# Nine Toeplitz products a head instead of ten, and two sums of each chunk pair on GpSimd

## The chip, the core and the metric

The kernel runs on one core of a Trainium2 chip, as one launch. The metric is the device time of the launch in microseconds (us). The engines are PE (TensorE, matmuls), DVE (VectorE), ACT (ScalarE), POOL (GpSimd) and SP (SyncE, which issues most of the DMAs). Each works through its own queue in order.

## What is computed

The input x has the shape (8, 256, 512), the context as well. Layer one is a causal long convolution with a product structure; layer two is a mixture of 16 experts with four experts a token, plus a shared expert. With k = v = context and q = layernorm(x), and 32 heads of 8 rows:

```python
kv = jnp.einsum('bhil,bhjl->bijhl', k_, v_)
y = jnp.fft.irfft(jnp.fft.rfft(kv, n=2 * L) * kernel_f, n=2 * L)[..., :L]
out = jnp.einsum('bijhl,bhil->bjhl', y + kv * D[None, None, None, :, None], q_)
x = x + out
x = x + ffn(layernorm(x))   # shared expert and 4 of 16 experts, each a gated silu
```

The convolution along L = 512 is causal. Cut into four chunks of 128, it is a lower triangular block Toeplitz product: with T0 to T3 the four 128 x 128 blocks of one head and K0 to K3 the chunks of kv, chunk c of y is the sum over m from 0 to c of Tm times K(c-m). That is 1 + 2 + 3 + 4 = 10 products.

## The kernel before

All is fp32. The attention part is one loop of 16 iterations over n. One iteration handles a tile of 128 rows (8 batches by 16 rows), which is two heads (HT = 2). Since k = v, only 288 of the pairs (i, j) are formed (PAIRS = 4 x 64 + 32), so one Toeplitz product is a 128x128 by 128x288 matmul.

- blocks (L345) loads the four Toeplitz blocks of a head from pad_d, a copy of the convolution kernel in device memory with 128 zeros ahead of it and D added to its first element. Partition p reads 512 consecutive values from an offset that grows by one with p. This is the DMA toep<-pad_d at L349: one contiguous piece of 2 KB for each partition. The blocks of an iteration are loaded by SP at the start of the one before; toep has four buffers.
- products (L354) forms kv on GpSimd: one instruction at L359 (128x128) and four at L361 (128x256) for a head. kv has four buffers.
- attend (L368) is called twice for a head, for chunks 0 and 1 (c0 = 0, three matmuls) and for chunks 2 and 3 (c0 = 2, seven). The matmuls at L381 accumulate in y, a PSUM tile with two buffers. DVE then multiplies y with q and sums over i: z at L393, L398 and L404, y in place at L409, f at L410, f with itself at L411 (128x256), and the sum into oT at L412 (128x128). y is free after L410; f and z have two buffers.
- add_to_x (L416) transposes oT of the iteration before on PE and adds it to x (L422). statistics (L262) runs on ACT with two small instructions on GpSimd, L273 and L274 (rstd); normalise (L290) is on ACT.
- From the fourth tile on, k and q of the next tile come in another layout through device memory: send_blocks (sent) and fetch_blocks (got) on SP, then a DVE transpose of 32 x 32 blocks (L327) and an ACT copy (L333). Up to the third tile, PE transposes them (heads_of, L336).
- by_feature (L440) computes the gate's logits of a finished tile on PE (L444), takes the four largest on DVE and counts selected tokens in early (L460, on DVE).
- shared_block (L137) is the shared expert as a generator; fill(count) runs so many of its pieces. These pieces (sgu at L163, sgt at L149, so at L180) are PE work put between the attends, and what is left of them after the loop runs on, before the experts start.

The order of each engine's instructions is the order in which the code issues them (manual_schedule over all engines). In an iteration that order is: DMA loads, attend(0, 0), fill, statistics of a later tile, attend(0, 2), add_to_x of the tile before, fill, the products of the next tile's head 0, attend(1, 0), fill, normalise and store of the tile before, the products of head 1, the gate of an older tile, attend(1, 2), fill, normalise of a later q.

PSUM is used in full: ps_mm two buffers for the shared expert, ps_tr two buffers (tag pt) for transposes and gate products, ps_y two of two banks each.

Of the kernel before, what the change touches and what calls it, by code (L numbers as in the profile page):

```python
# [20 lines left out]
P = 128  # L21
BK = 32
B, S, L = 8, 256, 512
HD = 8
# [12 lines left out]

ND = HD // 2
PAIRS = ND * HB + HB // 2
KW = HB + 3 * B  # L40
QW = HB + 4 * B
BACK = 2 * B
# [9 lines left out]
def ssm_attention__then__moe_kernel(  # L52
# [33 lines left out]

    xw_d = dram.tile([T + CAP, ROW], F32, name="xw_d")
    pad_d = dram.tile([S // HD, P + L], F32, name="pad_d")

    pad = const.tile([S // HD, P + L], F32, name="pad")
    dcol = const.tile([S // HD, 1], F32, name="dcol")
    nc.vector.memset(pad[:, 0:P], 0.0)
    nc.scalar.dma_start(out=pad[:, P:], in_=ssm)
    nc.scalar.dma_start(out=dcol, in_=skip)
    nc.vector.tensor_add(pad[:, P : P + 1], pad[:, P : P + 1], dcol)
    nc.scalar.dma_start(out=pad_d[:, :], in_=pad)  # L100
    ident = const.tile([P, P], F32, name="ident")
    make_identity(nc, ident)
    mhalf = const.tile([P, 1], F32, name="mhalf")
# [151 lines left out]
    with ExitStack() as att:  # L255
# [3 lines left out]
        work = att.enter_context(tc.tile_pool(name="work", bufs=2))  # L259
        ps_y = att.enter_context(tc.tile_pool(name="ps_y", bufs=2, space=PSUM))  # L260

        def statistics(dst, src, total=None):  # L262


            if total is None:
                total = small.tile([P, 1], F32, name="total")
                nc.scalar.activation(dst, src, AF.Identity, accum_out=total)
            neg = small.tile([P, 1], F32, name="neg")
            ss = small.tile([P, 1], F32, name="ss")
            rstd = small.tile([P, 1], F32, name="rstd")  # L270
# [73 lines left out]

        def blocks(head):  # L345

            toep = work.tile([P, L], F32, name="toep", bufs=4)
            row = pad_d[head : head + 1, 1 : 1 + L]
            nc.sync.dma_start(  # L349
                out=toep, in_=bass.AP(tensor=row.tensor, offset=row.offset, ap=[[1, P], [1, L]])  # L350
            )
            return toep

        def products(hh, k2):  # L354

            kv = work.tile([P, NC, PAIRS], F32, name="kv", bufs=4)
            kh = k2[:, :, hh, :]
            kc = kh.ap[1][0]
            nc.gpsimd.tensor_mul(kv[:, :, ND * HB :], kh[:, :, 0 : HB // 2], kh[:, :, HB // 2 : HB])  # L359
            for c in range(NC):  # L360
                nc.gpsimd.tensor_mul(  # L361
                    kv[:, c, 0 : ND * HB].rearrange("p (d w) -> p d w", d=ND),
                    kh[:, c, 0:HB].unsqueeze(1).broadcast_to([P, ND, HB]),
                    view(kh[:, c, :], 0, [[B, ND], [1, HB]]),
                )
            return kv

        def attend(hh, c0, toep, kv, q2, oT):  # L368

            qh = q2[:, :, hh, :]
            qc = qh.ap[1][0]
            y = ps_y.tile([P, 2, 512], F32, name="y")
            for i in range(2):
                c = c0 + i
                for m in range(c + 1):  # L380
                    nc.tensor.matmul(  # L381
                        y[:, i, 0:PAIRS],
                        lhsT=toep[:, m * P : (m + 1) * P],
                        rhs=kv[:, c - m, :],
                        start=(m == 0),
                        stop=(m == c),
                    )
# [15 lines left out]
            w = (ND - 1) * B  # L403
            nc.vector.tensor_mul(  # L404
                view(z, ZW, [[zc, 2], [ZW + B, ND - 1], [1, w]]),
                yd[:, :, 1:ND, HB - w : HB],
                qq[:, :, HB - w : HB].unsqueeze(2).broadcast_to([P, 2, ND - 1, w]),
            )
            nc.vector.tensor_mul(yd, yd, view(qq, 0, [[qc, 2], [B, ND], [1, HB]]))  # L409
            nc.vector.tensor_add(f, yd, z[:, :, :, BACK : BACK + HB])  # L410
            nc.vector.tensor_add(f[:, :, 0:2, :], f[:, :, 0:2, :], f[:, :, 2:4, :])  # L411
            nc.vector.tensor_add(  # L412
                oT[:, c0 : c0 + 2, hh * HB : (hh + 1) * HB], f[:, :, 0, :], f[:, :, 1, :]
            )

# [24 lines left out]
        def by_feature(n):  # L440
# [16 lines left out]

            if n == 0:
                nc.vector.memset(early[:, 0, :], 0.0)
            nc.vector.tensor_add(early[:, n + 1, :], early[:, n, :], sel[:, n, :])  # L460

        toeps = {}

# [29 lines left out]
        qn = load.tile([P, L], F32, name="qn", tag="kn")  # L493
        k2 = heads_of(loaded.pop(0), KW, "k2")
        stats = first_statistics(xs[:, 0, :])
        kvs = [products(0, k2)]
        normalise(qn, xs[:, 0, :], *stats)
        kvs.append(products(1, k2))
        q2 = heads_of(qn, QW, "q2")
        pg = ps_tr.tile([P, NC, P], F32, name="pg", tag="pt")  # L500
        for c in range(NC):
# [28 lines left out]
        for n in range(NT):  # L530
# [9 lines left out]
            if swift and more:  # L540
                got_k, got_q = fetch_blocks(sent_k), fetch_blocks(sent_q)
            load_shared(9)
            if n:
                attend(0, 0, tps[0], kvs[0], q2, oT)
            if n - 2 in MILD:
                transpose_blocks(xnT[:, :, n - 2, :], got_x)
            if more:
# [3 lines left out]
                        statistics(qn, xs[:, n + 1, :]) if n else first_statistics(xs[:, 1, :])  # L551
                    )
            if n == 0:
                attend(0, 0, tps[0], kvs[0], q2, oT)
            fill(2)
            if n + 2 in SWIFT:
                kp, kp_by_block = in_blocks("kp")
                kp_stats = statistics(kp_by_block, chunked(xs[:, n + 2, :]))

            attend(0, 2, tps[0], kvs[0], q2, oT)  # L560
            if more and not swift:
                k_next = heads_of(loaded.pop(n + 1), KW, "k2")
                normalise(qn, xs[:, n + 1, :], *stats)
# [5 lines left out]
            if more:  # L569
                if swift:  # L570
                    k_next = heads_from(got_k, KW, "k2")
                kv_next = [products(0, k_next)]

            attend(1, 0, tps[1], kvs[1], q2, oT)
            if more and not swift:
                q_next = heads_of(qn, QW, "q2")
            fill(2)
# [7 lines left out]
            if more:  # L585
                if swift:
                    q_next = heads_from(got_q, QW, "q2")
                kv_next.append(products(1, k_next))
            if n + 2 in SWIFT:
                nc.scalar.copy(kp_by_block, chunked(loaded.pop(n + 2)))  # L590
                sent_k = send_blocks(kp)
            if n - 2 in MILD:
                ready(n - 2)

            attend(1, 2, tps[1], kvs[1], q2, oT)
            if n - 1 in MILD:
                got_x = fetch_blocks(sent_x)
            elif n > 0:
# [320 lines left out]
```

## Time and profile before

| | |
|---|---|
| median of 3 runs | 717.03 us (716.22 to 719.62) |
| the profiled execution | 719.41 us |
| its span, first to last instruction | 717.7 us |
| mean granted TensorE clock | 0.99 |
| L361, products on GpSimd, 128x256, 128 of them | 698 ns median |
| L359, products on GpSimd, 128x128, 32 of them | 457 ns median |
| L409, y in place on DVE, 128x512, 64 of them | 700 ns mean |
| toep<-pad_d on SP, 32 of 256 KB | 4.8 us median from issue to landing |

The profiled execution's time is 1.7 us longer than its span, for what lies around the first and last instruction. The attention loop runs from about 11 to 370 us, what is left of the shared expert to about 445, the experts to the end. The first three iterations (to about 46 us) have little or no shared expert work to put between the attends. In the listings an instruction group is given as line, engine, operation, output<-inputs, shape and count, then busy time and the mean of one; answers for one line give the minimum, median and maximum instead.

### The profile page before, as it was taken

The page shows a single profiled execution, that of the slowest core. Times are in us where ns is not written, and L with a number is a line of the kernel's source. Part 1 is how long each engine was busy: PE and PEld are TensorE (multiplying, and loading weights), DVE is VectorE, ACT ScalarE, POOL GpSimd, SP SyncE. Part 2 cuts the span into 40 slices and gives each one's busy share as a digit, 9 for nine tenths or more (in the row PEclk, how much of TensorE's full clock was granted, in tenths as well). Part 3 has the DMA queues.
Part 4 walks back from the last instruction along what each step waited for, and adds up shares of the span by engine and source line. Part 5 has one row for each costly group of instructions (what it writes and reads, how often), then busy time and mean ns, then how long its engine had stood idle before and what let it go on. Part 6 is the DMA issues. An engine that isn't in the chain of part 4 may idle for free.

```text
span 717.7 us, 9733 instructions
## 1 busy us (share of the span) xinstructions
PE 692.0 (96%) x3471; PEld 521.5 (73%) x3471; DVE 402.3 (56%) x952; ACT 187.1 (26%) x472; POOL 211.8 (30%) x307
## 2 busy tenths in 40 slices
PE   5899999899999999999999999999999999999994
PEld 3677877787876886886876685777777677777772
DVE  3787767879987877778635511333333433443221
ACT  2353234352332351331122001121212221112120
POOL 5444224353333342133000020122332233332221
PEclk9999999999999999999999999999999999999997
DMA  7832453645556445541007431476677776777732
GB/s 202 290 89 75 118 148 80 175 126 158 144 155 162 108 117 143 148 106 55 16 16 241 116 86 30 133 213 182 182 192 219 213 193 185 200 203 207 195 42 32
DMA packets 76144, 102.17 MB, mean 142 GB/s; under 512 B 10224, under 2 KB 45040, under 8 KB 76096
## 3 DMA queue, kind: packets, MB, share of 16 engines
q1 hardware_dynamic: 68784, 84.35, 40.7%
q0 software_dynamic: 7168, 17.04, 11.6%
q8 instruction: 28, 0.46, 0.3%
q14 instruction: 20, 0.16, 0.1%
q10 hardware_dynamic: 144, 0.15, 0.1%
HBM read 74.02 MB, written 27.49 MB: 141 GB/s over the span
## 4 chain that ended last, share of the span: by engine, by line
PE 91%; DVE 4%; DMA 2%; issue 1%; ACT 1%; POOLq 0%; POOL 0%; ACTq 0%; DVEq 0%; SPq 0%
PE y L381 20%; PE sgu L163 19%; PE pgu L795 15%; PE eo L837 11%; PE so L180 11%; PE pgu L815 4%; PE pt L134 2%; PE pgu L807 2%; PE sgt L149 2%; PE lg L444 2%; PE ip L700 1%; PE pt L420 1%; DVE y L409 1%; DVE f L410 1%; DMA out<-eo_sb,idx 1%
## 5 line engine op out<-in xcount | busy, mean ns | idle before, releaser
L381 PE MATMUL y<-kv,toep 128*128 128x288 f32 x640 | 172.5, 419 | 3.0 <-DVE f L410 2.1
L381 PEld LDWEIGHTS y<-kv,toep 128*128 128x128 f32 x640 | 123.0, 196 | 41.2 <-issue 7.2
L795 PE MATMUL pgu<-xgT,w 128*128 128x256 f32 (+1 forms) x544 | 113.8, 367 | 0.8 <-ACT xgT L767 0.8
L795 PEld LDWEIGHTS pgu<-xgT,w 128*128 128x128 f32 x544 | 98.5, 190 | 20.4 <-issue 7.7
L361 POOL TENSOR_TENSOR kv<-k 128x256 f32<-128x256 f32 x128 | 88.9, 724 | 0.0
L837 PE MATMUL eo<-wd,mid 128*128 128x512 f32 (+1 forms) x192 | 86.4, 598 | 0.0
L846 POOL DMA_INDIRECT out<-eo_sb,idx x32 | 51.0, 1595 | 103.3 <-DMA out<-eo_sb,idx 73.2
L163 PE MATMUL sgu<-xnT,swg 128*128 128x256 f32 (+1 forms) x400 | 78.1, 338 | 2.4 <-DVE tail L157 2.4
L163 PE MATMUL sgu<-xnT,swu 128*128 128x256 f32 (+1 forms) x400 | 77.8, 337 | 0.0
L754 POOL DMA_INDIRECT g<-xw_d,idx x32 | 32.0, 999 | 150.7 <-PE eo L837 64.7
L180 PE MATMUL so<-swd,smid 128*128 128x512 f32 x160 | 74.4, 594 | 0.0
L273 POOL TENSOR_SCALAR rstd<-ss 128x1 f32<-128x1 f32 x30 | 5.8, 192 | 230.9 <-ACT xn L272 161.2
L163 PEld LDWEIGHTS sgu<-xnT,swg 128*128 128x128 f32 x400 | 65.3, 191 | 9.7 <-DVE tail L157 2.6
L163 PEld LDWEIGHTS sgu<-xnT,swu 128*128 128x128 f32 x400 | 64.7, 191 | 6.3
L837 PEld LDWEIGHTS eo<-wd,mid 128*128 128x128 f32 (+1 forms) x192 | 35.1, 190 | 37.9 <-issue 33.6
L803 DVE TENSOR_TENSOR mid<-eact,pgu 128x256 f32<-128x256 f32 (+1 forms) x34 | 13.8, 406 | 70.8 <-ACT eact L802 70.8
L393 DVE TENSOR_TENSOR z<-y,q 128x128 f32<-128x128 f32 x64 | 18.4, 287 | 61.6 <-PE y L381 61.4
L172 ACT ACTIVATE act<-sgu 128x256 f32<-128x256 f32 (+1 forms) x50 | 17.0, 341 | 136.4 <-PE sgu L163 134.9
L802 ACT ACTIVATE eact<-pgu 128x256 f32<-128x256 f32 (+1 forms) x34 | 12.6, 371 | 152.1 <-PE pgu L795 152.1
L180 PEld LDWEIGHTS so<-swd,smid 128*128 128x128 f32 x160 | 29.7, 190 | 31.0 <-issue 29.2
L845 DVE TENSOR_SCALAR eo_sb<-eo,g 128x512 f32<-128x512 f32 x32 | 24.0, 751 | 46.3 <-PE eo L837 46.3
L409 DVE TENSOR_TENSOR y<-y,q 128x512 f32<-128x512 f32 x64 | 44.8, 700 | 2.2
(149 smaller groups left out, 793.0 us busy)
## 6 DMA issues: line engine op xcount, KB each, us to landing
w<-in_L_ffn_w_gate SPq DMA_DIRECT2D x16, 704.0 KB, 4.4
w<-in_L_ffn_w_up SPq DMA_DIRECT2D x16, 704.0 KB
got<-sent SPq DMA_DIRECT2D x36, 256.0 KB, 5.2
toep<-pad_d SPq DMA_DIRECT2D x32, 256.0 KB, 4.8
wd<-in_L_ffn_w_down SPq DMA_DIRECT2D x16, 512.0 KB, 4.7
kn<-in_ctx SPq DMA_DIRECT2D x16, 256.0 KB, 5.2
xs<-in_x SPq DMA_DIRECT2D x16, 256.0 KB, 5.5
xw_d<-xn SPq DMA_DIRECT2D x16, 256.0 KB, 2.9
```

Source lines behind the costliest of these rows:

```text
L163: nc.tensor.matmul(pgu[:, k, :], lhsT=sw[:, c, f * P : (f + 1) * P], rhs=toks[:, c, :], start=(c == 0), stop=(c == NC - 1),)
L180: nc.tensor.matmul(po, lhsT=m[:, i * P : (i + 1) * P], rhs=swd[:, (f - 1) % (NF + 1), :], start=(f == 0), stop=(f == NF),)
L361: nc.gpsimd.tensor_mul(kv[:, c, 0 : ND * HB].rearrange("p (d w) -> p d w", d=ND), kh[:, c, 0:HB].unsqueeze(1).broadcast_to([P, ND, HB]), v ...
L381: nc.tensor.matmul(y[:, i, 0:PAIRS], lhsT=toep[:, m * P : (m + 1) * P], rhs=kv[:, c - m, :], start=(m == 0), stop=(m == c),)
L393: nc.vector.tensor_mul(z[:, :, 0, BACK : BACK + HB].rearrange("p i (h w) -> p i h w", h=2), y[:, :, ND * HB : PAIRS].unsqueeze(2).broadcas ...
L409: nc.vector.tensor_mul(yd, yd, view(qq, 0, [[qc, 2], [B, ND], [1, HB]]))
L754: nc.gpsimd.indirect_dma_start(out=g, out_offset=None, in_=xw_d[:, :], in_offset=bass.IndirectOffsetOnAxis(ap=idx[:, e, n : n + 1], axis=0),)
L795: nc.tensor.matmul(pgu[:, k, cols], lhsT=w[:, k, c, f * P : (f + 1) * P], rhs=xgT[:, c, cols], start=(c == 0), stop=(c == NC - 1),)
L815: nc.tensor.matmul(pgu[:, 0, cols], lhsT=wt[:, c, 0:P], rhs=xgT[:, c, cols], start=(c == 0), stop=(c == NC - 1),)
L837: nc.tensor.matmul(po, lhsT=mid[:m, f, n * P : (n + 1) * P], rhs=wd[:m, f, :], start=(f == 0), stop=(f == NI - 1),)
L845: nc.vector.tensor_scalar_mul(o, po, g[:, L + e : L + e + 1])
L846: nc.gpsimd.indirect_dma_start(out=out, out_offset=bass.IndirectOffsetOnAxis(ap=idx[:, e, n : n + 1], axis=0), in_=o, in_offset=None, comp ...
```

## The change

A constant PLAIN = 6 splits the heads. Heads 0 to 5 (the first three iterations) are computed as before. For heads 6 to 31, the second attend writes

- y2 = T0 K2 + (T1 - T2) K1 + T2 (K0 + K1), and
- y3 = T0 K3 + T1 K2 + (T3 - T2) K0 + T2 (K0 + K1),

so T2 (K0 + K1) is computed once, in a tile shared that takes a ps_tr buffer; ACT copies it to SBUF (again), and DVE adds it to both halves of y in place. That makes six matmuls there instead of seven, nine a head.

The operands come with it. products sums chunks 0 and 1 of kv on GpSimd as a fifth chunk, and kv has three buffers. windows, called once in the second iteration, forms the differences of blocks on GpSimd (less) and writes five windows of 256 values for each head to win_d; blocks then loads 5 x 128 values for each partition, in five pieces of 512 B. The tile pad moves from a buffer of its own to a k2 buffer, and its loads are issued a few lines later.

The last two sums of attend (L411 and L412) go to GpSimd for heads 6 to 31, both chunk pairs; so does the sum of early in by_feature, for all tiles.

```diff
...
+PLAIN = 3 * 2
...
     xw_d = dram.tile([T + CAP, ROW], F32, name="xw_d")
     pad_d = dram.tile([S // HD, P + L], F32, name="pad_d")
-    pad = const.tile([S // HD, P + L], F32, name="pad")
-    dcol = const.tile([S // HD, 1], F32, name="dcol")
-    nc.vector.memset(pad[:, 0:P], 0.0)
-    nc.scalar.dma_start(out=pad[:, P:], in_=ssm)
-    nc.scalar.dma_start(out=dcol, in_=skip)
-    nc.vector.tensor_add(pad[:, P : P + 1], pad[:, P : P + 1], dcol)
-    nc.scalar.dma_start(out=pad_d[:, :], in_=pad)
+    win_d = dram.tile([S // HD, 5, 2 * P], F32, name="win_d")
     ident = const.tile([P, P], F32, name="ident")
     make_identity(nc, ident)
     mhalf = const.tile([P, 1], F32, name="mhalf")
...
         work = att.enter_context(tc.tile_pool(name="work", bufs=2))
         ps_y = att.enter_context(tc.tile_pool(name="ps_y", bufs=2, space=PSUM))
+        pad = half.tile([S // HD, P + L], F32, name="pad", tag="k2")
+        dcol = const.tile([S // HD, 1], F32, name="dcol")
+        nc.vector.memset(pad[:, 0:P], 0.0)
+        nc.scalar.dma_start(out=pad[:, P:], in_=ssm)
+        nc.scalar.dma_start(out=dcol, in_=skip)
+        nc.vector.tensor_add(pad[:, P : P + 1], pad[:, P : P + 1], dcol)
+        nc.scalar.dma_start(out=pad_d[:, :], in_=pad)
+        def windows():
+            less = load.tile([S // HD, 2, 2 * P], F32, name="less", tag="kn")
+            for i, m in enumerate((1, 3)):
+                nc.gpsimd.tensor_sub(
+                    less[:, i, :], pad[:, m * P : (m + 2) * P], pad[:, 2 * P : 4 * P]
+                )
+            nc.sync.dma_start(out=win_d[:, 0:3, :], in_=view(pad, 0, [[P, 3], [1, 2 * P]]))
+            nc.sync.dma_start(out=win_d[:, 3:5, :], in_=less)
         def statistics(dst, src, total=None):
...
         def blocks(head):
-            toep = work.tile([P, L], F32, name="toep", bufs=4)
-            row = pad_d[head : head + 1, 1 : 1 + L]
+            if head < PLAIN:
+                toep = work.tile([P, L], F32, name="toep", bufs=4)
+                row = pad_d[head : head + 1, 1 : 1 + L]
+                dims = [[1, P], [1, L]]
+            else:
+                toep = work.tile([P, 5, P], F32, name="toep", bufs=4)
+                row = win_d[head : head + 1, 0, 1 : 1 + P]
+                dims = [[1, P], [2 * P, 5], [1, P]]
             nc.sync.dma_start(
-                out=toep, in_=bass.AP(tensor=row.tensor, offset=row.offset, ap=[[1, P], [1, L]])
-            )
-            return toep
-        def products(hh, k2):
-            kv = work.tile([P, NC, PAIRS], F32, name="kv", bufs=4)
+                out=toep, in_=bass.AP(tensor=row.tensor, offset=row.offset, ap=dims)
+            )
+            return toep if head < PLAIN else toep.rearrange("p m q -> p (m q)")
+        def products(head, hh, k2):
+            kv = work.tile([P, NC + 1, PAIRS], F32, name="kv", bufs=3)
             kh = k2[:, :, hh, :]
             kc = kh.ap[1][0]
-            nc.gpsimd.tensor_mul(kv[:, :, ND * HB :], kh[:, :, 0 : HB // 2], kh[:, :, HB // 2 : HB])
+            nc.gpsimd.tensor_mul(kv[:, 0:NC, ND * HB :], kh[:, :, 0 : HB // 2], kh[:, :, HB // 2 : HB])
             for c in range(NC):
                 nc.gpsimd.tensor_mul(
                     kv[:, c, 0 : ND * HB].rearrange("p (d w) -> p d w", d=ND),
                     kh[:, c, 0:HB].unsqueeze(1).broadcast_to([P, ND, HB]),
                     view(kh[:, c, :], 0, [[B, ND], [1, HB]]),
                 )
+            if head >= PLAIN:
+                nc.gpsimd.tensor_add(kv[:, NC, :], kv[:, 0, :], kv[:, 1, :])
             return kv
-        def attend(hh, c0, toep, kv, q2, oT):
+        def attend(head, hh, c0, toep, kv, q2, oT):
...
             qh = q2[:, :, hh, :]
             qc = qh.ap[1][0]
             y = ps_y.tile([P, 2, 512], F32, name="y")
-            for i in range(2):
-                c = c0 + i
-                for m in range(c + 1):
+            def convolve(out, pairs):
+                for n, (m, rhs) in enumerate(pairs):
                     nc.tensor.matmul(
-                        y[:, i, 0:PAIRS],
+                        out,
                         lhsT=toep[:, m * P : (m + 1) * P],
-                        rhs=kv[:, c - m, :],
-                        start=(m == 0),
-                        stop=(m == c),
+                        rhs=rhs,
+                        start=(n == 0),
+                        stop=(n == len(pairs) - 1),
                     )
+            if c0 == 0 or head < PLAIN:
+                for i in range(2):
+                    c = c0 + i
+                    convolve(y[:, i, 0:PAIRS], [(m, kv[:, c - m, :]) for m in range(c + 1)])
+            else:
+                shared = ps_tr.tile([P, PAIRS], F32, name="shared", tag="pt")
+                convolve(shared, [(2, kv[:, NC, :])])
+                again = work.tile([P, PAIRS], F32, name="again", bufs=1)
+                nc.scalar.copy(again, shared)
+                convolve(y[:, 0, 0:PAIRS], [(0, kv[:, 2, :]), (3, kv[:, 1, :])])
+                convolve(
+                    y[:, 1, 0:PAIRS], [(0, kv[:, 3, :]), (1, kv[:, 2, :]), (4, kv[:, 0, :])]
+                )
+                nc.vector.tensor_add(
+                    y[:, :, 0:PAIRS],
+                    y[:, :, 0:PAIRS],
+                    again.unsqueeze(1).broadcast_to([P, 2, PAIRS]),
+                )
             z = work.tile([P, 2, ND, ZW], F32, name="z")
             f = work.tile([P, 2, ND, HB], F32, name="f")
             zc = z.ap[1][0]
...
             )
             nc.vector.tensor_mul(yd, yd, view(qq, 0, [[qc, 2], [B, ND], [1, HB]]))
             nc.vector.tensor_add(f, yd, z[:, :, :, BACK : BACK + HB])
-            nc.vector.tensor_add(f[:, :, 0:2, :], f[:, :, 0:2, :], f[:, :, 2:4, :])
-            nc.vector.tensor_add(
+            adder = nc.vector if head < PLAIN else nc.gpsimd
+            adder.tensor_add(f[:, :, 0:2, :], f[:, :, 0:2, :], f[:, :, 2:4, :])
+            adder.tensor_add(
                 oT[:, c0 : c0 + 2, hh * HB : (hh + 1) * HB], f[:, :, 0, :], f[:, :, 1, :]
             )
...
             if n == 0:
                 nc.vector.memset(early[:, 0, :], 0.0)
-            nc.vector.tensor_add(early[:, n + 1, :], early[:, n, :], sel[:, n, :])
+            nc.gpsimd.tensor_add(early[:, n + 1, :], early[:, n, :], sel[:, n, :])
         toeps = {}
...
         qn = load.tile([P, L], F32, name="qn", tag="kn")
         k2 = heads_of(loaded.pop(0), KW, "k2")
         stats = first_statistics(xs[:, 0, :])
-        kvs = [products(0, k2)]
+        kvs = [products(0, 0, k2)]
         normalise(qn, xs[:, 0, :], *stats)
-        kvs.append(products(1, k2))
+        kvs.append(products(1, 1, k2))
         q2 = heads_of(qn, QW, "q2")
         pg = ps_tr.tile([P, NC, P], F32, name="pg", tag="pt")
         for c in range(NC):
...
+            if n == 1:
+                windows()
             if n:
-                attend(0, 0, tps[0], kvs[0], q2, oT)
+                attend(n * HT + 0, 0, 0, tps[0], kvs[0], q2, oT)
...
```

The other calls of products and attend change in the same way: they pass the number of the head as a first argument.

More of the change, by code (lines that the diff above doesn't have):

```diff
@@ L553, in ssm_attention__then__moe_kernel @@
             if n == 0:
-                attend(0, 0, tps[0], kvs[0], q2, oT)
+                attend(n * HT + 0, 0, 0, tps[0], kvs[0], q2, oT)
             fill(2)
@@ L558, in ssm_attention__then__moe_kernel @@
                 kp_stats = statistics(kp_by_block, chunked(xs[:, n + 2, :]))
-            attend(0, 2, tps[0], kvs[0], q2, oT)
+            attend(n * HT + 0, 0, 2, tps[0], kvs[0], q2, oT)
             if more and not swift:
@@ L571, in ssm_attention__then__moe_kernel @@
                     k_next = heads_from(got_k, KW, "k2")
-                kv_next = [products(0, k_next)]
-            attend(1, 0, tps[1], kvs[1], q2, oT)
+                kv_next = [products((n + 1) * HT, 0, k_next)]
+            attend(n * HT + 1, 1, 0, tps[1], kvs[1], q2, oT)
             if more and not swift:
@@ L587, in ssm_attention__then__moe_kernel @@
                     q_next = heads_from(got_q, QW, "q2")
-                kv_next.append(products(1, k_next))
+                kv_next.append(products((n + 1) * HT + 1, 1, k_next))
             if n + 2 in SWIFT:
@@ L593, in ssm_attention__then__moe_kernel @@
                 ready(n - 2)
-            attend(1, 2, tps[1], kvs[1], q2, oT)
+            attend(n * HT + 1, 1, 2, tps[1], kvs[1], q2, oT)
             if n - 1 in MILD:
```

## The prediction, made before the result was known

> **What bounds the kernel now.** I read the page's busy table first, then the chain that ended last, then the chain and the waits inside the attention loop, because the change touches nothing outside that loop. These lines carry it:
>
> ```profile
> PE 692.0 (96%) x3471; PEld 521.5 (73%) x3471; DVE 402.3 (56%) x952; ACT 187.1 (26%) x472; POOL 211.8 (30%) x307
> ...
> PE 91%; DVE 4%; DMA 2%; issue 1%; ACT 1%; POOLq 0%; POOL 0%; ACTq 0%; DVEq 0%; SPq 0%
> ```
>
> A busy PE alone proves little (matmul ends are modelled), but the chain agrees: 91% of the span is PE following PE. In the loop, by stretch of about one iteration (two heads; columns PE, PEld, DVE, ACT, POOL busy, granted clock, DMA share, GB/s):
>
> ```profile
> 121.50:142.00 20.50, 18.12 (x87) 13.43 (x86) 16.87 (x41) 6.52 (x16) 7.82 (x14) 1.00 0.61 170
> ...
> 176.00:198.30 22.30, 22.30 (x105) 18.63 (x104) 21.28 (x61) 9.47 (x25) 10.68 (x19) 1.00 0.54 147
> ...
> 221.40:244.50 23.10, 23.10 (x97) 17.26 (x97) 18.57 (x43) 6.08 (x16) 7.82 (x14) 1.00 0.62 152
> ```
>
> A steady iteration is 23.1 us, all PE; DVE has 4.5 us to spare, GpSimd 15. DVE is nearly full only around 176 to 198, where the masks are built, and PE does not wait even there. The waits of PE from 46 to 365 us are a single line:
>
> ```profile
> PE sgu L163 <- DVE tail L157: 2.4, 1, 2.4
> ```
>
> That is the hole in the first stretch, where DVE worked without a pause from 127.5 to 141.8. The chain of the iteration at 221.4 shows the two Toeplitz groups:
>
> ```profile
> 223.10 1.46 PE y L381 x6
> 224.56 3.43 PE so L180 x8
> 227.99 3.40 PE y L381 x14
> ```
>
> An fp32 matmul leaves two records here (640 for 32 heads of 10), so x6 is a first chunk pair of 3 products and x14 a second of 7: 3.40 / 7 = 0.486 us of PE for one product. The mean of 419 ns in the groups is one record, overlapping its neighbour, and is not used.
>
> **What the Trainium skill says.** "SBUF — State Buffer", Who interferes with whom: a DVE instruction with two SBUF inputs contends with a GpSimd instruction that reads SBUF, one waiting for the other; with one SBUF input it does not. The trace agrees: the two f sums (both inputs in SBUF) have medians of 425 and 293 ns but means and maxima well above; y<-y,q, which reads PSUM, keeps to 698 to 700 ns.
>
> ```profile
> L411 DVE TENSOR_TENSOR f<-f x64: 424/425/999, 17.1 to 364.6; 128x256 f32<-128x256 f32 x64
> L412 DVE TENSOR_TENSOR oT<-f x64: 291/293/683, 17.5 to 365.1; 128x128 f32<-128x128 f32 x64
> ```
>
> "GPSIMD Engine Reference", Performance versus the Vector engine: a two-input elementwise operation is about 2 times slower on GpSimd. Here 698 ns (median of 128x256) against 425 ns. "DMA: Bandwidth & Descriptors", Specifications: pieces of 512 B or more are needed for line rate; the new loads have pieces of exactly 512 B. I price that from the trace below.
>
> **The change part by part.**
>
> PE. Heads 6 to 31 (26 heads) do six products instead of seven in the second chunk pair: 26 x 0.486 = 12.6 us less. Nothing is added on PE. Since PE runs without a hole there, and the work it does between (shared-expert pieces) is a fixed list, a microsecond less of work is a microsecond less of time, as long as no operand comes late. After the loop the same leftover pieces follow without a hole, so the gain is carried to the end.
>
> DVE, per changed head. Gone: two 128x256 sums (mean 516) and two 128x128 sums (393), 1.82 us; of it 1.44 is work (medians) and 0.38 waiting for GpSimd. New: one sum of 2x288 in place in PSUM. The nearest row is y<-y,q, PSUM and SBUF in, PSUM out, 512 elements, 700 ns; at about 1.04 ns an element for 64 more, 0.77 us. Net -1.05 us a head (-0.67 without the lost waiting). The sum of early also leaves DVE (416 ns mean, once an iteration). So DVE goes from 18.5 to about 16.0 us an iteration while PE goes from 23.1 to 22.1. But the new sum lies ahead of everything that reads y, in the second pair only. Behind it on DVE are the five instructions of the same attend, then smid, the transposes of k and q, and the sum into xs. Who waits: PE for y's buffer (two of them), freed by f<-y,z. At 231.4 the second pair ends and DVE frees y 2.5 us later; PE wants that buffer at 241.0. Another 0.77 us is covered by 7 us. Cost nothing; if that cover were gone, 26 x 0.77 = 20 us.
>
> The copy of the shared product on ACT: PSUM to SBUF, 288 elements, from 375 ns at 256 elements 0.40 us; ACT is busy 6 to 10 us of 23. It comes after the shared product, PE's first of six, and must land while PE does the other five (2.4 us). Ahead of it on ACT: the statistics of kp (0.62 + 0.19 + 0.20 + 0.72 + 0.19 = 1.9 us) after a Silu, or the copies of q and kp (1.0 us). So it lands about when PE finishes: 0 to 0.3 us late for DVE, which 7 us covers. Behind it on ACT are the statistics and the normalised xn, which wait for DVE anyway. The shared tile takes a transpose buffer (two) that the next transpose of oT or the gate product wants 3 us later.
>
> GpSimd. The products stay: 457 + 4 x 698 ns a head. New a head: the sum of two chunks, 288 elements, 698 + 32 x 1.9 = 0.76 us; two sums of 256 (0.70) and two of 128 (0.46), 2.31 us. 3.07 us a head, 6.1 an iteration, 0.25 for early: 7.8 + 6.4 = 14.2 us of 22.1. Its queue is in order, so it now follows DVE's f instead of running ahead; behind a sum that waits are the rstd of the statistics and the next products. By the order written, the products of the next head 0 stand before the third attend and are wanted a head's time later (more than 5 us); an rstd is at most 1.2 us later, and its users are ACT's normalisations, gated by Silu or by DVE. f has two buffers: DVE's f of the next but one attend comes 8 us or more later. oT is read by PE about 6 us after GpSimd would finish. kv with three buffers instead of four: the fourth allocation reuses a tile last read by the second pair of head 0, already done. Cost nothing.
>
> DMA. toep goes from 128 pieces of 2 KB to 640 pieces of 512 B. In two stretches with 512 B packets alone the share of 16 engines gives the price: 242.6 to 244.8, 2.2 x 16 x 0.658 / 707 = 33 ns.
>
> ```profile
> DMA packets 707, 0.32 MB, mean 146 GB/s; under 512 B 81, under 2 KB 707, under 8 KB 707
> ...
> q1 hardware_dynamic: 707, 0.32, 65.8%
> ```
>
> A 2 KB packet takes 3.0 x 16 x 1.0 / 516 = 94 ns (253 to 256). A pair of toeps goes from 256 x 94 / 16 = 1.5 us to 1280 x 33 / 16 = 2.6; with 48 ns for reads that start off a boundary, 3.8. So 1 to 2.3 us later for what is behind them on SP's queue: kn, xs, and got for k and q. SP's time for issuing 640 pieces is not shown; 0.4 us now, I allow up to 2 each. got lands 4 to 6 us after its issue at 228.2, and DVE transposes k at 235.6: some waits of 1 to 2 us will appear on DVE, within its 6 us of slack.
>
> Start. The pad chain (1.2 to 11.3 us) keeps its length. windows() adds two GpSimd subtractions of 256 (1.4 us) where GpSimd idles near 28 us, and two small DMAs on SP behind the last shared weights, read first in the next iteration. pad borrows a k2 buffer; if the third k2 takes that very one, its copy at 35.5 would wait for those DMAs until about 38: 0 to 2.5 us. I take 0.3, as another k2 buffer is free by then.
>
> The 2.4 us hole: of DVE's 14.3 us there, two second pairs cost 0.04 each more, the first pair between loses 1.14 and early 0.62, so 1.7 less; PE comes 0.5 earlier. The hole shrinks by 1.2 (0 to 2.4).
>
> Sum: 12.6 + 1.2 - 0.3 = 13.5 us off the profiled execution, 719.4 to 705.9 us. The median shown, 717.0, is 2.4 below that execution; I take the same 13.5 (1.9%) off it: 703.5 us.
>
> **The rivals.**
> A, the forecast: 703.5, own range 701.5 to 706; 0.64.
> B, part is lost: the new links DVE-GpSimd-DVE, ACT-DVE and late got make PE wait 0.25 us a head on average (26 x 0.25 = 6.5), or the start loses 2.5 and the hole stays. 707 to 712. For it: DVE near full around 176; against: 7 us of cover. 0.20.
> C, hidden: DVE sets the pace instead and PE's saving becomes its waiting; 717. It needs DVE at 23 us an iteration where I count 16. 0.06.
> D, slower: GpSimd becomes the pace. Place: the loop of 13 iterations. It decides when its sum passes 23.1 us, so when the added 6.4 cost over 15.3, 2.4 times my price, through strided views or waiting. At 3 times: 7.8 + 19.2 = 27 us, 3.9 x 13 = 51 us longer; just past the point, at 2.6 times, 24.4 us and 17 us longer: 734. For it: the engine is the slow one and now in order behind DVE. Against: rows of the same shapes, and DVE's two-SBUF sums, which blocked it, are gone from those heads. 0.10.
>
> **How the numbers follow.** 0.5% (3.6 us) is about what a measurement of this kernel can tell from no change. A and B are faster: 0.84; C same: 0.06; D slower: 0.10. The range holds A and most of B: 700.5 to 711.
>
> **What would show it.** Right: Toeplitz records fall from 640 to 588, x14 groups become 12 records of 2.9 us; PE's idle in the loop stays under 3 us; DVE's busy falls by some 34 us (27 and 7 for early), GpSimd's rises by about 85, its iteration stays under 16 us; the two sums left on DVE (12 of 64) are all that spread. Wrong: PE waiting on y for f, on kv for GpSimd, on a transpose buffer for ACT, or iterations longer than 22.3 us.

## The result, and the profile after

| | before | after |
|---|---|---|
| median | 718.15 us (716.22 to 719.62, 4 runs) | 709.11 us (705.56 to 710.82, 4 runs) |
| profiled execution | 719.41 us | 708.86 us |
| its span | 717.7 us | 707.1 us |
| mean granted clock | 0.990 | 0.988 |
| first gate product to first expert product on PE | 43.44 to 446.47: 403.0 us | 40.36 to 435.81: 395.5 us |

The ratio is 0.9869, 95% interval 0.9822 to 0.9916: 1.3% faster where 1.9% was forecast. (The kernel before has one run more here than ahead of the prediction, so its median is 718.15 and no longer 717.03.) The last row is the stretch that the change touches, since heads 6 to 31 begin after the first gate product. It gains 7.6 us, where the forecast had 12.6 + 1.2 = 13.8. The other 3.1 us between the two profiled executions lie ahead of the first gate product, and so of every changed head. 1.7 us of it is a spell of slower clock that only the kernel before has there: read in steps of 1 us, the clock was 0.50 for 3.4 us from 31 on. Kernels with the same start as the kernel after reach that product between 40.35 and 44.65 us in the runs below, so I compare the stretch of the last row, not spans.

Both stretches hold one more such spell just behind the first gate product (from 44.7 before, from 41.8 after). In the first, fifth, eighth and tenth runs below it came between 28 and 33 us and lies ahead of the stretch, which is 1.7 us shorter for that alone: from the first to the second gate product it is 24.83 us in the first run and 26.51 in the kernel after. Where I compare these runs, the 1.7 us are taken into account.

The page of the kernel after, busy time and chain:

```profile
PE 679.8 (96%) x3419; PEld 512.1 (72%) x3419; DVE 371.4 (53%) x858; ACT 195.3 (28%) x498; POOL 294.1 (42%) x455
...
PE 90%; DVE 4%; DMA 3%; issue 1%; ACT 1%; SPq 0%; POOLq 0%; POOL 0%; ACTq 0%; DVEq 0%
```

PE still sets the end; DVE has lost 30.9 us and GpSimd gained 82.3, near the forecast 34 and 85. DMA's share of the chain went from 2% to 3%. The waits of PE from 46 to 365 us, one line before, are now three (line waited for, us in total, times, longest):

```profile
PE sgu L155 <- DVE tail L149: 1.8, 1, 1.8
PE shared L404 <- DVE xs L467: 1.4, 1, 1.4
...
PE y L404 <- DVE f L454: 0.6, 1, 0.6
```

All three name DVE, and all three lie between 130 and 168 us. The timeline of PE in the kernel after, at the first of them (start, us, line, output<-inputs, count, and in brackets the idle time before):

```profile
122.19 1.88 PE L172 MATMUL so<-swd,smid 128*128 128x512 f32 x4
123.91 1.62 PE L404 MATMUL y<-kv,toep 128*128 128x288 f32 x6
125.36 0.96 PE L489 MATMUL lg<-gwT,xnT 128*128 128x16 f32 x8
126.17 0.73 PE L404 MATMUL shared<-kv,toep 128*128 128x288 f32 x2
126.74 2.59 PE L404 MATMUL y<-kv,toep 128*128 128x288 f32 x10
129.17 1.05 PE L141 MATMUL sgt<-xnT,swt 128*128 128x128 f32 x8
130.81 1.69 PE L404 MATMUL y<-kv,toep 128*128 128x288 f32 x6 [0.59 <-DVE f L454]
```

Between the two chunk pairs of the second head (123.91 and 126.17) there is no piece of the shared expert at all, only the gate product of 0.8 us: the pieces of the finished blocks are used up, and the next block is not ready. The two attends of a head, the transposes and the next attend follow each other at PE's speed, and DVE has to keep up. The chain of waits of the kernel after in the same place (start, us, what):

```profile
121.56 5.87 DMA got<-sent
...
127.46 0.71 DVE k L340
...
129.86 0.69 DVE f L454
130.55 0.63 DVE q L340
...
132.13 0.30 ACT again L422
...
132.46 0.78 DVE y L427
...
135.79 0.30 DVE tail L149
...
136.13 2.03 PE sgu L155 x13
```

A late load (got), then DVE with one pause of 0.26 us (for ACT's copy, again) up to the release of the buffer that PE wants (tail), with the new 0.78 us sum in it. The second place, 40 us later, in the same view:

```profile
160.43 0.48 PE shared L404 x2
160.92 2.44 PE y L404 x10
...
163.45 0.78 DVE y L427
...
166.06 0.69 DVE f L454
166.75 0.61 DVE xs L467 x2
...
167.41 0.75 PE shared L404 x2
168.16 4.11 PE y L404 x10
```

Here the shared product of the next head waits for a transpose buffer, which DVE frees (xs) only behind the six instructions of the second pair, the new sum first. Then the same five products take 4.11 us instead of 2.44, with nothing to wait for. The clock explains that, by the stretches of the kernel after (us; PE, PEld, DVE, ACT, POOL busy; granted clock; DMA share; GB/s):

```profile
160.40:167.40 7.00, 5.63 (x31) 4.54 (x29) 5.82 (x13) 0.41 (x2) 3.66 (x13) 1.00 1.01 251
167.40:172.30 4.90, 4.89 (x13) 3.63 (x14) 4.59 (x13) 4.10 (x11) 4.30 (x9) 0.65 0.17 46
```

The missing 6.2 us of the stretch can be added up. The waits are 3.8 us in place of 2.4, where 1.2 was forecast: 2.6. Work at the low clock: behind the first wait the sgu group took 2.67 us, the shared product 0.96 and the Toeplitz group 3.01; behind the second the shared product took 0.75 and the Toeplitz group 4.11. The first run below had the same waits with the clock at 1.00, and its chain shows what the same groups cost then:

```profile
136.37 2.05 PE sgu L155 x16
138.42 0.49 PE shared L404 x2
138.91 2.42 PE y L404 x10
...
165.97 0.75 PE shared L404 x2
166.72 2.42 PE y L404 x10
```

The difference is 0.62 + 0.47 + 0.59 + 0 + 1.69 = 3.4 us for the clock. A group right behind a wait starts slower at full clock as well (2.05 where sgu takes 1.78 elsewhere, 0.75 where shared takes 0.48); the kernel before had this once, so it adds some 0.3 here. Together 6.3.

### The profile page after: what moved, and what is told of

It reads as the page before. It is cut to its first block, busy times and chain, and to the rows that moved or that the text cites. A ratio compares the mean times of both kernels' runs of the same rounds, so it can differ in the third digit from the quotient of the medians.

```text
span 707.1 us, 9801 instructions
## 1 busy us (share of the span) xinstructions
PE 679.8 (96%) x3419; PEld 512.1 (72%) x3419; DVE 371.4 (53%) x858; ACT 195.3 (28%) x498; POOL 294.1 (42%) x455
## 4 chain that ended last, share of the span: by engine, by line
PE 90%; DVE 4%; DMA 3%; issue 1%; ACT 1%; SPq 0%; POOLq 0%; POOL 0%; ACTq 0%; DVEq 0%
PE sgu L155 20%; PE y L404 16%; PE pgu L842 15%; PE eo L884 12%; PE so L172 11%; PE pgu L862 4%; PE pt L126 2%; PE pgu L854 2%; PE shared L404 2%; PE sgt L141 2%; PE lg L489 2%; PE ip L747 1%; DMA got<-sent 1%; DVE y L453 1%; PE pt L465 1%; DVE f L454 1%
## 5 line engine op out<-in xcount | busy, mean ns | idle before, releaser
L404 PE MATMUL y<-kv,toep 128*128 128x288 f32 x536 | 145.8, 418 | 3.6 <-POOL rstd L286 2.1
L404 PEld LDWEIGHTS y<-kv,toep 128*128 128x128 f32 x536 | 104.1, 197 | 36.6 <-issue 5.0
L381 POOL TENSOR_TENSOR kv<-k 128x256 f32<-128x256 f32 x128 | 86.6, 707 | 0.0
L456 POOL TENSOR_TENSOR f<-f 128x256 f32<-128x256 f32 x52 | 37.9, 728 | 94.6 <-DVE f L454 89.5
L849 ACT ACTIVATE eact<-pgu 128x256 f32<-128x256 f32 (+1 forms) x34 | 12.6, 371 | 152.1 <-PE pgu L842 152.1
L850 DVE TENSOR_TENSOR mid<-eact,pgu 128x256 f32<-128x256 f32 (+1 forms) x34 | 13.8, 406 | 70.8 <-ACT eact L849 70.8
L454 DVE TENSOR_TENSOR f<-y,z 128x512 f32<-128x512 f32 x64 | 44.3, 692 | 5.7
L427 DVE TENSOR_TENSOR y<-y,again 128x576 f32<-128x576 f32 x26 | 19.9, 766 | 51.4 <-PE y L404 48.6
```

What stands on the lines that cost most here:

```text
L381: nc.gpsimd.tensor_mul(kv[:, c, 0 : ND * HB].rearrange("p (d w) -> p d w", d=ND), kh[:, c, 0:HB].unsqueeze(1).broadcast_to([P, ND, HB]), v ...
L404: nc.tensor.matmul(out, lhsT=toep[:, m * P : (m + 1) * P], rhs=rhs, start=(n == 0), stop=(n == len(pairs) - 1),)
L456: adder.tensor_add(f[:, :, 0:2, :], f[:, :, 0:2, :], f[:, :, 2:4, :])
```

## The experiments

Three readings were tried: theory 1, got comes late because the blocks now come in small pieces; theory 2, PE waits for the transpose buffer that the shared product borrows, so another order of DVE's work should help; and theory 3, that the pieces of the shared expert run out in two iterations (n = 5 and 7), so that DVE's work, longer by the new sum, has no cover there. Runs are counted in the order in which they stand here. Intervals are of the ratio to the kernel before on the same chip. The kernel before had medians of 717.0 us beside the first four, 719.3 beside the next four, 717.3 beside the ninth to the eleventh and 719.9 beside the last, so ratios are compared, not times.

**Blocks in one piece a partition**

```diff
-                toep = work.tile([P, 5, P], F32, name="toep", bufs=4)
+                toep = work.tile([P, 5 * P], F32, name="toep", bufs=4)
-                dims = [[1, P], [2 * P, 5], [1, P]]
+                dims = [[1, P], [1, 5 * P]]
```

> The changed kernel, but toep of heads 6 to 31 is read as one piece of 2560 B for each partition instead of five of 512 B: as many bytes, a fifth of the packets, the same matmuls; the Toeplitz blocks read for those heads are other ones, so the attention of these heads is left out in its right form. Theory 1 (the missing 5 us in the loop between 115 and 180 us come from got landing late behind the many small pieces): DVE's wait for got (4.6 us in the changed kernel) falls under 1 us, PE's waits in the loop fall from 3.8 to about 2, and the kernel is 1.5 to 4 us faster than the changed one (705 to 707.5). Theory 2 (PE waits for the PSUM buffer that the shared product takes from the transposes): the wait of PE for DVE's sum into xs (1.4 us) stays, time within 1 us of the changed kernel (709).

706.32 us, ratio 0.9844 (0.9810 to 0.9879). The interval overlaps that of the change, and the three waits are the same (1.8, 1.4, 0.6). DVE's wait for got fell from 4.6 to 1.4 us. The stretch took 390.4 us, 5.1 less than in the kernel after, but the clock was 1.00 from 120 to 180 us, which accounts for 3.4 of it, and the spell of the start lay ahead of the stretch, which accounts for the other 1.7. So the time lies where theory 1 put it, but not for its reason: the small pieces are not what makes PE wait.

**got fetched ahead of the blocks**

```diff
+            if swift and more:
+                got_k, got_q = fetch_blocks(sent_k), fetch_blocks(sent_q)
             if more:
                 for hh in range(HT):
                     load_blocks((n + 1) * HT + hh)
...
-            if swift and more:
-                got_k, got_q = fetch_blocks(sent_k), fetch_blocks(sent_q)
```

> The changed kernel, but got for k and q is issued on SP ahead of toep, kn and xs, which have an iteration or more of time. Theory 1: got lands 3 to 5 us earlier, DVE's wait for it is gone, and PE's waits in the loop fall to about 2 us; 705 to 707. Theory 2: PE still waits 1.4 us or more for DVE's sum into xs and the clock still sinks after it; within 1 us of 709. If SP is held up by waiting for the last sent, toep comes later and PE waits for toep: slower.

705.70 us, 0.9836 (0.9799 to 0.9872). got now lands 2.8 us after its issue; this is its line on the page:

```profile
got<-sent SPq DMA_DIRECT2D x36, 256.0 KB, 2.8
```

It was 6.0 in the kernel after and 5.2 before. DVE waited for it (before the transposes of k) 4.6 us in the kernel after, five times, at most 1.3, and never here. Yet PE's two longer waits hardly move: 1.7 us for tail and 1.4 for xs, where they were 1.8 and 1.4; only the 0.6 for y is gone. The stretch took 391.1 us, 4.4 less than in the kernel after, and 3.4 of that is again the clock, at 1.00 from 120 to 180 us.

The late load was real and stood in the chain, but behind it DVE's own work was already the limit. What it is worth (0.3% by medians) this comparison can't tell from nothing.

**The two parts alone.** First nine products with all sums on DVE:

```diff
-            adder = nc.vector if head < PLAIN else nc.gpsimd
+            adder = nc.vector
...
-            nc.gpsimd.tensor_add(early[:, n + 1, :], early[:, n, :], sel[:, n, :])
+            nc.vector.tensor_add(early[:, n + 1, :], early[:, n, :], sel[:, n, :])
```

> The changed kernel with the last two sums of each chunk pair and early back on DVE; nine products stay. DVE gets 26 x 1.44 = 37 us of work more and waits for GpSimd again. If DVE's load decides in the stretch from 115 to 180 us (both theories ask for DVE in time), PE's waits there grow from 3.8 us to 8 or more: 713 to 717. If the sums do not matter to PE, 709 within 1 us.

715.71 us, 0.9961 (0.9940 to 0.9982). The same two waits of PE, doubled:

```profile
PE sgu L155 <- DVE tail L149: 4.0, 1, 4.0
PE shared L404 <- DVE xs L467: 3.1, 2, 2.6
```

The clock was 0.69 in the 10 us from 140 and 0.68 in those from 170. Then ten products as before, and only the sums of heads 6 to 31 and of early on GpSimd:

```diff
-            nc.vector.tensor_add(f[:, :, 0:2, :], f[:, :, 0:2, :], f[:, :, 2:4, :])
-            nc.vector.tensor_add(
+            adder = nc.vector if plain else nc.gpsimd
+            adder.tensor_add(f[:, :, 0:2, :], f[:, :, 0:2, :], f[:, :, 2:4, :])
+            adder.tensor_add(
```

> The kernel before (ten products) with the two sums of heads 6 to 31 and early moved to GpSimd, nothing else. DVE loses 26 x 1.8 us. The only PE wait of the loop there is the 2.4 us hole; so 0 to 2.7 us faster than before (715.5 to 718). If GpSimd's order costs anything, slower than before and PE waits for kv or oT.

714.07 us, 0.9954 (0.9939 to 0.9969). Of the waits only the first gate product's is left, so the old hole of 2.4 us is gone:

```profile
PE lg L445 <- ACT xnT L600: 0.7, 1, 0.7
```

The stretch is 400.3 us, 2.7 less than before, with the spell of the start in both. So each part alone brings some 0.4 to 0.5% and both 1.3%: the move is what makes room on DVE for the sum that the nine products need.

**Other orders on DVE.** add_to_x ahead of the second attend from the fifth iteration on, so that the transpose buffer comes free before the six instructions; then with got fetched first as well; then also the transposes of k moved ahead:

```diff
+            if n > 3:
+                total = add_to_x(n - 1, oT_done)
             attend(n * HT + 0, 0, 2, tps[0], kvs[0], q2, oT)
...
-            if n > 0:
+            if 0 < n < 4:
                 total = add_to_x(n - 1, oT_done)
```

> The changed kernel, but from the fifth iteration on add_to_x (the transposes of oT on PE and DVE's sum into xs) is issued ahead of the second chunk pair of head 0 instead of behind it, so the transpose's PSUM buffer is free long before the second shared product asks for it. Theory 2 (the PSUM buffer): PE's wait for DVE's sum into xs (1.4 us) is gone, DVE does that sum where it idled before, and the wait for tail shrinks too; PE's waits from 46 to 365 us fall from 3.8 to under 2, time 705 to 707.5. Theory 1 (got): DVE's wait for got stays (3 us or more), the wait of PE for tail stays at 1.8; 708 to 710. If oT is not ready that early, PE waits for GpSimd's sum and the kernel is slower than the changed one.

> Both edits: got ahead of toep, and add_to_x ahead of the second chunk pair of head 0. If the two waits are separate and all that is left, PE's waits in the loop fall under 1 us and the time is the forecast of the PE sum alone: before less 12.6 less the 2.4 us hole, 701 to 703.5. If a third thing holds DVE (the new sum in y on DVE itself), about 1.7 us of wait for tail stays: 704 to 705.

> As the run before, and the transposes of k by DVE stand ahead of the second chunk pair too, from the fifth iteration on. Takes 0.7 us more out of DVE's stretch behind that pair: the wait for tail is gone, 701 to 703. If got is not there yet at that point, DVE waits for it and PE for y: slower than the run before.

711.40 us, 0.9902 (0.9864 to 0.9939); 710.07, 0.9877 (0.9845 to 0.9909); 712.42, 0.9906 (0.9872 to 0.9941). None is better than the change. In the first PE waits for GpSimd's sum, as the last case of its expectation had it, though that it is slower than the change isn't shown. The second missed, with 6.2 us of waiting of PE where less than 1 was expected. The waits of PE in the first of them:

```profile
PE pt L465 <- POOL oT L457: 2.9, 1, 2.9
PE sgu L155 <- DVE tail L149: 1.8, 1, 1.8
PE y L404 <- DVE f L454: 1.7, 2, 1.0
```

The wait for xs is gone and one for GpSimd has come: the sums that finish oT now stand on GpSimd behind the products of the next head, and the earlier transposes meet them. These three are the only runs in which GpSimd holds PE up in the loop.

**The shared product left out of chunks 2 and 3** (neither copied nor added, so y2 and y3 lack T2 (K0 + K1)):

```diff
-                again = work.tile([P, PAIRS], F32, name="again", bufs=1)
-                nc.scalar.copy(again, shared)
...
-                nc.vector.tensor_add(
-                    y[:, :, 0:PAIRS],
-                    y[:, :, 0:PAIRS],
-                    again.unsqueeze(1).broadcast_to([P, 2, PAIRS]),
-                )
```

> The changed kernel without ACT's copy of the shared product and without DVE's sum of it into y; this leaves the shared product out of chunks 2 and 3. DVE has 20 us less. If DVE's new sum is what delays PE where the filling is short, all PE waits in the loop are gone and the time is 701 to 703. If got or the PSUM buffer holds PE on their own, 1.4 us or more of wait stays and the time is 705 or more.

704.41 us, 0.9809 (0.9774 to 0.9844); the stretch 388.4 us, or 390.1 with the spell of the start in it. The waits of this kernel:

```profile
PE sgu L155 <- DVE tail L149: 0.7, 1, 0.7
...
PE y L404 <- DVE f L447: 0.6, 1, 0.6
PE shared L404 <- DVE xs L460: 0.5, 1, 0.5
```

The waits for tail and xs fall from 3.2 us to 1.2, and the clock stays at 1.00 behind them. The sum in place (20 us of DVE in all) and the copy ahead of it cost PE about 2 us of waiting, in those two places. With the 3.4 us of clock this makes up the 5.3 us by which the stretch is shorter than in the kernel after. Which of the two instructions it is, this run can't tell, as it leaves out both.

**The pieces spread evenly.** One piece fewer behind add_to_x up to n = 7, and none ahead of the first gate products (which n = 1 to 3 have there), so that pieces are left for n = 5 to 8:

```diff
-            fill(2)
+            fill(1 if n < 8 else 2)
...
-                fill(1)
+                if n > 8:
+                    fill(1)
                 ready(n - 1)
```

> The changed kernel with the shared-expert pieces spread: up to the eighth iteration one piece instead of two behind the second chunk pair of head 0, and none ahead of the gate of the first tiles; the pieces left over run after the loop. Theory 3 (the first two theories name only what comes last; what is short is PE work between the attends in the iterations near 120 and 165 us, where the pieces have run out and DVE, with 0.77 us more to do in each second pair, cannot follow): all PE waits between 46 and 365 us are gone (under 0.7 us), the clock stays at 1.00 there, time 702 to 705. Theories 1 and 2: got and the PSUM buffer still hold PE, 2 us of wait or more, 706 to 709.

> The spread pieces and got ahead of toep. Theory 3: as the run before within 0.5 us, since a late got is covered once DVE has time: 702 to 704.5, with no PE wait in the loop. If late got costs by itself, 1 us or more faster than the run before. Against the kernel with ten products and the sums on GpSimd (714.1, no PE wait in its loop) the nine products should give their full 26 x 0.486 = 12.6 us.

The second also fetches got first. 705.40 us, 0.9814 (0.9773 to 0.9854), and 703.40 us, 0.9790 (0.9761 to 0.9820). No wait for DVE is left. What is left is waits for ACT's copy of xnT, which the expectation did not have. The longest in the waits of the second, after which there is only one of 0.7 us for xn, which others had too:

```profile
PE lg L489 <- ACT xnT L646: 2.0, 3, 0.7
```

Its stretch is 387.9 us, 12.4 less than with the move alone (400.3, also without a hole), against 12.6 for 26 products of 0.486. But 1.7 of the 12.4 is the spell of the start, which lay ahead of the stretch here and in it there, so 10.7 can be put down to the products. The waits for xnT are 1.3 us longer here. The ninth run, with the spell in its stretch, took 389.6, which is the same as the tenth with 1.7 added: once PE has other work in the two places, fetching got first brings nothing in these two profiles.

**The same with the sums on DVE** (the edit of the third run on top of the tenth):

> As the run before, but the two sums and early back on DVE, so that nine products stand without the move to GpSimd. DVE needs about 19.5 us an iteration against 19 to 22 of PE. If the spread alone is enough, 703 to 705; if DVE's load decides, PE waits of 3 us or more stay in the stretch from 100 to 200 us and the time is 707 to 713.

713.28 us, 0.9909 (0.9875 to 0.9943). The stretch from 100 to 200 us of this kernel, by engine, and PE's waits:

```profile
100.00:200.00 100.00, 97.11 (x501) 77.06 (x500) 90.31 (x219) 41.71 (x112) 45.89 (x85) 1.00 0.57 148
```

```profile
PE lg L489 <- ACT xnT L646: 3.1, 3, 1.8
PE sgu L155 <- DVE tail L149: 2.7, 3, 1.6
```

DVE is busy 90 of 100 us, so pieces between the attends no longer cover it. The move is needed, and so is the spreading.

**A piece kept ahead of the gate products.** As the tenth run, but with that piece kept, and dropped behind the second pair of head 1 for n = 2 and 3 instead:

```diff
                 ready(n - 1)
-            fill(1)
+            if n not in (2, 3):
+                fill(1)
```

> As e10_even_got, but the one piece of the shared expert ahead of the first gate products is kept in every head, as in the changed kernel; to have as many pieces left, heads 2 and 3 leave out the piece behind the second chunk pair of head 1 instead. In e10 PE waits three times for ACT's copy of xnT, 2.0 us together; in the changed kernel it waits 0.7 us there. Theory 3 (it is the number of pieces left for heads 5 to 8 that matters, and a piece ahead of the gate products covers the copy of xnT): the wait falls back to 0.7 us, no wait for the tail comes back, and the time is 702 to 703 us, 0.4 to 1.3 below e10. Rival (the waits for xnT are hidden by the rest, or the pieces are missed where they were dropped): 703.4 us within 0.5, or above 704.5 if a wait for the tail of a chunk comes in heads 2 and 3.

702.94 us, 0.9765 (0.9739 to 0.9791): the fastest, and its interval lies below that of the change (0.9822 to 0.9916). Of the waits of this kernel the first, and its stretch from 100 to 200 us:

```profile
PE lg L489 <- ACT xnT L646: 0.7, 1, 0.7
```

```profile
100.00:200.00 100.00, 100.00 (x521) 80.63 (x520) 78.02 (x187) 42.23 (x112) 71.13 (x133) 1.00 0.59 152
```

The waits fell as expected. The stretch took 387.7 us, with the spell of the start in it: 12.7 less than with the move alone, which had the spell in its stretch and one wait of 0.7 us for xnT as well. The 12.6 us of the 26 products are there in full. Against the tenth run it is 1.9 us less with the spell taken into account, 1.3 of it in the waits; the times of the two kernels alone (702.94 and 703.40) don't show a difference. In the place where the kernel after had no piece, PE's timeline of this kernel now has four half groups (pieces with gates and ups, 119.98 to 123.56) between the pairs of the second head:

```profile
118.53 1.62 PE L404 MATMUL y<-kv,toep 128*128 128x288 f32 x6
119.98 1.05 PE L155 MATMUL sgu<-xnT,swg 128*128 128x128 f32 x8
...
122.66 1.06 PE L155 MATMUL sgu<-xnT,swu 128*128 128x128 f32 x8
...
124.37 0.73 PE L404 MATMUL shared<-kv,toep 128*128 128x288 f32 x2
```

## Where the prediction held and where it didn't

The direction and the main term held. The forecast gain of 13.5 us was 9.0 by medians. The measured time lies in the wide range, but only because that was drawn to take in most of rival B: the forecast itself, A, with its own range of 701.5 to 706, missed.

- PE: right. 588 Toeplitz records, and a second pair of 2.42 + 0.48 = 2.90 us in place of 3.40.
- DVE: right in size. The sum in place took 766 ns (forecast 0.77), and the 12 sums left there are the only ones that still spread:

```profile
L456 POOL TENSOR_TENSOR f<-f x52: 716/728/743, 73.7 to 354.9; 128x256 f32<-128x256 f32 x52
L456 DVE TENSOR_TENSOR f<-f x12: 424/426/978, 17.1 to 67.4; 128x256 f32<-128x256 f32 x12
```

  In this answer for one line of the kernel after (minimum, median and maximum in ns), GpSimd's own time keeps within 4%, while DVE's reaches 978: as the Trainium skill ("SBUF — State Buffer", Who interferes with whom) has it, sums with two SBUF inputs can be held up on DVE.
- ACT: the copy took 390 ns (forecast 0.40). DVE waited for it 2.8 us in three places, once 2.3 (at 112.9) where 0.3 was the most allowed; no wait of PE follows there.
- GpSimd: right. 728 and 458 ns (0.70 and 0.46 forecast); 15.4 us in the 23 us from 217 and 13.6 in the 22 from 240, where 14.2 an iteration was forecast. Rival D fell; rival C too, over the loop as a whole.
- DMA: right. toep landed in 5.1 us instead of 4.8, got in 6.0 instead of 5.2. DVE waited for got at most 1.3 us at a time, and SP issued a block of 640 pieces in 0.43 us (median). The stretch from which 33 ns a packet was read did not hold pieces of 512 B alone, as its line shows: 81 of the 707 were smaller.
- Start: no cost seen.
- The step that failed is "Another 0.77 us is covered by 7 us. Cost nothing". The 7 us were read at 231 to 241, in a steady iteration, and taken for all. At 119 to 136 and 160 to 172 the pieces that give the cover are used up. With it fell "The hole shrinks by 1.2": it shrank by 0.6, and waits of 1.4 and 0.6 came, for the transpose buffer that the shared product borrows and for y. The prediction named who wants that buffer 3 us later, but not that the next shared product waits in its turn for DVE to free one. Rival B had the mechanism (new links on DVE make PE wait) and the outcome (707 to 712), but as 0.25 us a head; it was 3.8 us of waiting in two iterations, and 3.4 of slower clock behind it, which neither A nor B had. That the sum came out within B's 707 to 712 is luck. From the twelfth run, which has the products' 12.6 us in full, it follows that nothing was lost elsewhere.

The thin cover could have been read in the trace of before: its timeline has, between the pairs of the same head, the gate product alone.

```profile
129.40 1.62 PE L381 MATMUL y<-kv,toep 128*128 128x288 f32 x6
130.86 0.96 PE L444 MATMUL lg<-gwT,xnT 128*128 128x16 f32 x8
131.67 3.64 PE L381 MATMUL y<-kv,toep 128*128 128x288 f32 x14
```

## What to carry to other kernels

Cover that is read from one steady iteration holds for that iteration. Where filler work is handed out from a list, look for the iterations in which the list is empty, and price an added instruction on the second engine there. A change that makes the leading engine faster need not move these places (the bare one of head 11 was there before and after), but it leaves the engine behind it less time in them. Spreading the filler, got's order included, then brought as much as the change itself had: 7.8 us of the stretch, against 7.6. What spreading brings to ten products was not run; the only wait of PE for DVE there was the 2.4 us hole.

## What was not expected of the hardware

The granted clock fell at waits of PE of only 1.4 to 4.0 us (the kernel after, the third run). Read in steps of 1 us it is 0.50 in these spells, for 3.4 us each in the kernel after (from 137.4 and from 168.1) and for 6.8 us each in the third run (from 139.4 and from 173.5); the 0.65 to 0.69 above are means of longer stretches. The Trainium skill ("TensorE: Matmul & The Clock Gate", What's actually happening) puts the fall after an idle window of some 3.4 us and lets that window run freely. The length of the spells agrees with that window; a wait of 1.4 us is shorter than it. That the window runs freely would suit the rest. Waits of the same length left the clock at 1.00 in the first and second runs, and one of 2.4 us did in the kernel before. A wait of 2.9 us met a spell in the sixth run and none in the seventh; in the eleventh one of 1.8 us brought a spell (92 to 96 us) and one of 1.6 did not. When a wait brings the slower clock and when not isn't settled by these runs. In the kernel after it made the loss 6.3 us instead of 2.9, and it may be why that kernel's four runs spread from 705.56 to 710.82: the fastest had a mean clock of 0.993, the other three of 0.988.
